# A hybrid layer on one Trainium2 core: queries of the second attention projected with features on partitions

## The chip, the core and the metric

The kernel runs on one core of one Trainium2 chip. The time is that of one execution on the device, in microseconds (us), and the figure compared is the median of several runs. The kernel before has a median of 1133.28 us over 3 runs (1132.96 to 1135.29).

## What is computed

The input x holds 2 batches of 1024 tokens with 512 features, all fp32. Four blocks are added to it in turn, each on a layer-normalised copy:

```python
x = x + attention_a(layernorm(x))
x = x + ffn(layernorm(x))
x = x + attention_b(layernorm(x))
x = x + ffn(layernorm(x))
```

Attention A is a causal differential attention with 16 heads, whose output is filtered along the tokens, scaled per head and projected. The FFN has 8 small experts of 16 inner features, of which each token uses the best 2. Both are left as they are. Attention B is the block in question:

```python
h = _layernorm(X, ln_w, ln_b)
Q, K, V = jnp.split(h @ W_in + b_in, 3, axis=-1)
Q, K = _rope_half(Q), _rope_half(K)        # pairs 2i, 2i+1 of the first 256 features are rotated
A = jnp.sum(_cos_sim(K) * V, axis=-2)      # one row of 512 per batch
Y = (A[:, None, :] * Q) @ W_out + b_out
return Y + X
```

K and V are used only within a token and in a sum over tokens. Q is multiplied by one row A and then by W_out. So the kernel scales the rows of W_out by A once per batch (it calls the result ws) and multiplies q by ws, for which q must have its features on partitions.

## The kernel before

**Tiles.** The 2048 tokens are 16 tiles of 128 (NTILE), 8 for each batch (JT); the 512 features are 4 chunks of 128 (EC). x stays on the chip as x_sb. TensorE takes a stationary operand of 128 x 128 and a moving one; one matmul in fp32 leaves two records in the profile, so a product of 128 x 512 by 512 x 512 (4 matmuls with 512 columns moving) shows as "x8".

**Two stages.** The first stage, up to about 711 us, is attention A without the end of its second half. It isn't touched. The second stage (lines 932 to 1451) is a loop `for t in range(NTILE + 2)` and a tail behind it. In a step t the loop does: the head norm and the output projection of attention A for a later tile (head_norm, mixed, projected; its sums tp_y, yT, z), every few steps products with the filter (common, apart; y), the first FFN of tile t (expert_turn, expert_hidden, expert_gate, expert_back, up; tp_f, xT_f, hr_f, sg_f, atp_f, aT_f, po_f), the layer norm of attention B for tile t-1 (attn_norm, attn_sides, attn_turn; hn_b, tp_b, hT_b) and the projections of attention B for tile t-2 (attn_qk, attn_v, attn_add, accumulate, attn_q). From t=10 it also makes the sums of batch 0 (attn_sum(0)) and one tile of output a step (attn_out; py). From t=13 the second FFN begins, on groups of tiles, and the tail finishes batch 1.

**What sets the order.** The loop stands in `tc.manual_schedule(engines=ordered)`: TensorE, VectorE (DVE) and ScalarE (ACT) execute their instructions in the order in which the Python code writes them. GpSimd (POOL) and SyncE (SP, which issues the loads) may be ordered by the scheduler. Each engine's queue is served in order: an instruction that waits holds up all that stand behind it. Buffers come from pools: six banks of PSUM called "wide" for products, two banks called "tp" for transposes, 8 buffers for QT, 4 for fxT (the turned input of the FFN), 4 for y, one for hT.

**The path of q before.** attn_qk(n, 0) at line 1240 projects q with tokens on partitions (attn_project, line 1236: stationary hT of the tile, moving 512 columns of W_in), adds the bias on VectorE (line 1243) and rotates (rope, lines 1228 to 1231: two products on VectorE, one on POOL, a sum on POOL; pairs lie next to each other, so each product reads every second element). The result qkv_q waits until the end of the step. There attn_q (line 1271) turns it: four transposes on TensorE into a "tp" bank (tp_q, line 970) and one copy on ScalarE into QT (line 975). k takes the same path without the turning. attn_out (line 1296) multiplies QT by ws into py and adds py to x_sb.

**The sums.** attn_sum (line 1279) adds the accumulated row over partitions by TensorE (pc, line 1283), copies it to acol on VectorE (line 1285), and scales W_out by it, two chunks on VectorE (line 1292) and two on ScalarE (line 1294). In step 10 it stands before; that is, behind expert_turn(10), whose last instruction is the copy xT_f on ScalarE (line 1091), and ahead of attn_qk(8, 0). Then follow expert_hidden (hr_f, line 1104), attn_out(0), attn_out(1), attn_v.

Of the kernel before, what the change touches and what calls it, by code (L numbers as in the profile page):

```python
# [11 lines left out]
F32 = mybir.dt.float32  # L12
BF16 = mybir.dt.bfloat16
AF = mybir.ActivationFunctionType
ALU = mybir.AluOpType
# [3 lines left out]
P = 128  # L19
NB, T, E = 2, 1024, 512  # L20
NT = NB * T
JT = T // P
NTILE = NT // P
EC = E // P
# [5 lines left out]
TILE = [b * JT + q + k for b in range(NB) for q in range(2) for k in (0, 4, 2, 6)]  # L30
# [5 lines left out]
def constants():  # L36

    f = np.float32
    t = np.arange(T, dtype=f)

    def tiled(a):
        return np.ascontiguousarray(a.reshape(JT, P, -1).transpose(1, 0, 2).reshape(P, -1))

    inv = (f(1.0) / np.power(f(10000.0), np.arange(0, HD, 2, dtype=f) / f(HD))).astype(f)
    fr = np.outer(t, inv).astype(f)


    r = np.arange(P)
    part = np.where(r // 2 % 2, f(1.0), f(-(HD**-0.5)))[:, None]
    sign = np.where(r % 2, f(1.0), f(-1.0))[:, None]  # L50
    rope_a = np.concatenate([part * np.cos(fr).T[r // 4 % 8], part * sign * np.sin(fr).T[r // 4 % 8]], axis=1).astype(f)

    rot = E // 2
    inv = (f(1.0) / np.power(f(10000.0), np.arange(0, rot, 2, dtype=f) / f(rot))).astype(f)
    fr = (t[:, None] * inv[None, :]).astype(f)
    rope_b = np.concatenate([tiled(np.cos(fr)), tiled(np.sin(fr))], axis=1).astype(f)

    x = np.linspace(0.0, 1.0, T // 2 + 1)  # L60
    taps = np.fft.irfft(np.exp(-0.5 * (x / 0.15) ** 2), n=T)
    lag = (128 * np.arange(JT)[None, :, None] + np.arange(P)[None, None, :] - np.arange(P)[:, None, None]) % T

    block = [taps[lag[:, d]] for d in range(JT)]
    sums = [(block[d] + block[d + 4]) / 2 for d in range(4)]
    parts = [(sums[d] + sums[d + 2]) / 2 for d in range(2)]
    parts += [(sums[d % 4] - sums[(d + 2) % 4]) / 2 for d in range(-1, 2)]
    parts += [(block[d % JT] - block[(d + 4) % JT]) / 2 for d in range(-3, 4)]  # L70
    filt_k = np.concatenate(parts, axis=1).astype(f)


    tri = np.tile(np.tril(np.ones((NE, NE), f), -1).reshape(1, -1), (P, 1))
    return {"c_rope_a": rope_a, "c_rope_b": rope_b, "c_filt": filt_k, "c_tri": tri}


@with_exitstack
def hybrid_layer_kernel(ctx: ExitStack, tc: tile.TileContext, i: dict, out: bass.AP):
    nc = tc.nc  # L80
# [66 lines left out]
    with ExitStack() as sa:  # L147
# [8 lines left out]
        with ExitStack() as sp:  # L156
# [6 lines left out]
            work = sp.enter_context(tc.tile_pool(name="work", bufs=2))  # L163
# [768 lines left out]
        with ExitStack() as sb:  # L932
# [5 lines left out]
            def load_b(name, src, shape):  # L938
                t = wb.tile(shape, F32, tag=name, name=f"{name}_sb")
                nc.sync.dma_start(t, src)  # L940
                return t
# [6 lines left out]
                "rope_b", i["c_rope_b"].rearrange("p (s j f) -> p s j f", s=2, j=JT), [P, 2, JT, E // 4]  # L948
            )
            wob = load_b("wob", i["W_out"].rearrange("(c p) f -> p c f", p=P), [P, EC, E])  # L950
            bias = wb.tile([P, 3 * E], F32, tag="bias", name="bias_sb")
            nc.sync.dma_start(bias, i["b_in"].partition_broadcast(P))
            bout = wb.tile([P, E], F32, tag="bout", name="bout_sb")
            nc.sync.dma_start(bout, i["b_out"].partition_broadcast(P))
            one = wb.tile([P, 1], F32, tag="one", name="one")
# [2 lines left out]
            def wide(name):  # L958
                return ps_w.tile([P, 512], F32, tag="wide", name=name)
# [4 lines left out]
            def w2k(name, tag, bufs=2):  # L964
                return work.tile([P, E], F32, tag=tag, name=name, bufs=bufs)
# [7 lines left out]
            def transposed(dst, src, key):  # L973

                nc.scalar.copy(dst, transposes(src, key))
# [106 lines left out]
            def expert_turn(ns, which):  # L1082
                for n in ns[:2]:
                    expert_scale(n)
                for k, n in enumerate(ns):
                    key = f"f{which}_{n}"
                    xTs[n] = work.tile([P, EC, P], F32, tag="fxT", name=f"xT_{key}", bufs=4)
                    turned = transposes(xns.pop(n), key)
                    if k + 2 < len(ns):
                        expert_scale(ns[k + 2])  # L1090
                    nc.scalar.copy(xTs[n], turned)
# [128 lines left out]

            def rope(t, j, key):

                left = t[:, 0 : E // 2].rearrange("p (f s) -> p f s", s=2)
                cos = rope_b[:, 0, j, :, None].to_broadcast([P, E // 4, 2])
                sin = rope_b[:, 1, j, :]
                ra = work.tile([P, E // 4, 2], F32, tag="ra", name=f"ra_{key}")
                rb = work.tile([P, E // 4, 2], F32, tag="rb", name=f"rb_{key}")
                nc.vector.tensor_mul(ra, left, cos)
                nc.vector.scalar_tensor_tensor(rb[:, :, 0], left[:, :, 1], -1.0, sin, ALU.mult, ALU.mult)
                nc.gpsimd.tensor_mul(rb[:, :, 1], left[:, :, 0], sin)  # L1230
                nc.gpsimd.tensor_add(left, ra, rb)

            def attn_project(n, s):
                pq = wide(f"pq_{'qkv'[s]}{n}")
                for c in range(EC):
                    nc.tensor.matmul(pq, hTs[n][:, c, :], win(c, s), start=(c == 0), stop=(c == EC - 1))  # L1236
                return pq

            def attn_qk(n, s):
                key = f"{'qk'[s]}{n}"  # L1240
                pq = attn_project(n, s)
                t = qkvs[n, s] = w2k(f"qkv_{key}", f"qkv{s}")
                nc.vector.tensor_add(t, pq, bias[:, s * E : (s + 1) * E])
                rope(t, TILE[n] % JT, key)

            def attn_v(n):

# [5 lines left out]
            def attn_add(n):  # L1253

                pq, n2, r0 = qkvs.pop((n, 2))
                rn = rsqrt_step(n2, r0, 1, f"n{n}")
                t = w2k(f"qkv_v{n}", "qkv2", bufs=1)
                nc.vector.tensor_add(t, pq, bias[:, 2 * E : 3 * E])  # L1258
                nc.gpsimd.tensor_mul(t, t, qkvs[n, 1])  # L1259
                qkvs[n, 2] = t, rn  # L1260

            def accumulate(n):
# [4 lines left out]
                    nc.vector.tensor_scalar_mul(acc[b], t, rn)  # L1267
                else:
                    nc.vector.scalar_tensor_tensor(acc[b], t, rn, acc[b], ALU.mult, ALU.add)

            def attn_q(n):
                QTs[n] = work.tile([P, EC, P], F32, tag="QT", name=f"QT_{n}", bufs=8)
                transposed(QTs[n], qkvs[n, 0], f"q{n}")


            group = [0, 1, 2, 3]
            pair = [[n, n + 1] for n in range(4, 16, 2)]
# [1 line left out]
            def attn_sum(b):  # L1279

                pc = wide(f"pc_{b}")
                for c in range(EC):
                    nc.tensor.matmul(pc[:, c : c + 1], acc[b][:, c * P : (c + 1) * P], one, start=True, stop=True)
                col = stat.tile([P, EC], F32, tag="acol", name=f"acol_{b}")
                nc.vector.tensor_copy(col, pc[:, 0:EC])

                if b == 0:
                    wss["both"] = keep.tile([P, JT, E], F32, tag="folded0", name="ws")
                wss[b] = wss["both"][:, EC * b : EC * b + EC, :]
                for c in range(EC):  # L1290
                    if c % 2 == 0:
                        nc.vector.tensor_scalar_mul(wss[b][:, c, :], wob[:, c, :], col[:, c : c + 1])
                    else:
                        nc.scalar.activation(wss[b][:, c, :], wob[:, c, :], AF.Copy, scale=col[:, c : c + 1])

            def attn_out(n):
                py = wide(f"py_{n}")
                for c in range(EC):
                    nc.tensor.matmul(py, QTs[n][:, c, :], wss[n // JT][:, c, :], start=(c == 0), stop=(c == EC - 1))  # L1299
                nc.vector.tensor_add(x_sb[:, n, :], x_sb[:, n, :], py)  # L1300
                ns = group if n < 4 else pair[n // 2 - 2]
                group_moments(ns, ns.index(n))

            with tc.manual_schedule(engines=ordered):
                for t in range(NTILE + 2):

                    def due(what, n, *args, listed=False):
                        if 0 <= n < NTILE:
                            what([n] if listed else n, *args)
# [41 lines left out]
                    if mixing and t > 2:  # L1351
                        due(up, t - 1, 0, listed=True)
                        due(attn_norm, t - 1)
                    due(attn_qk, t - 2, 1)
                    if not mixing:
                        due(expert_back, t - 1, 0, listed=True)
                    if t == 0:
                        expert_turn([2], 0)
                    if t > 2:
                        due(expert_turn, t, 0, listed=True)  # L1360
                    if t == 10:
                        attn_sum(0)
                    if t == 14:
                        expert_turn(group, 1)
                    if t == 17:
                        expert_turn(pair[0], 1)
                        group_norm(pair[1])
                    due(attn_qk, t - 2, 0)
                    if not mixing:
                        due(up, t - 1, 0, listed=True)  # L1370
                        if t != 15:
# [7 lines left out]
                        attn_norm(t - 1)  # L1379
                    if t == 10:  # L1380
                        attn_out(0)
                    if 10 <= t < 17:
                        attn_out(t - 9)
                    due(attn_sides, t - 1)
# [15 lines left out]
                    due(attn_add, t - 2)  # L1400
                    if turned is not None:
                        projected(turned)
                    due(attn_q, t - 2)
                    if t == 14:
                        expert_gate(group, 1)
                    if t == 13:
# [79 lines left out]
```

## Time and profile before

| | us |
|---|---|
| median of 3 runs | 1133.28 |
| the profiled execution | 1133.31 |
| its span, from first to last instruction | 1131.2 |
| second stage, from 711 to the end of the span | 420 |

| group of the second stage (from 741 us on) | records | busy us |
|---|---|---|
| pq_q, line 1236 | 128 | 57.7 |
| tp_q, line 970 | 64 | 9.6 |
| tp_y, line 970 | 44 | 6.8, with 1.7 idle ahead, released by ACT QT |
| py, line 1299 | 128 | 57.0 |

How to read it. The mean granted clock of TensorE is 0.992 of full. "Busy" of TensorE adds up records of which the ends are modelled; consecutive matmuls overlap, so what one costs is read from the distance between starts. A line of the timeline has the start in us, the busy time, the engine, the line of the kernel, the operation, output and inputs with their shapes, a count, and in brackets the idle time ahead of it with what ended it. A line of the windows has the window, its length, the busy time of TensorE, its weight loads (PEld), VectorE, ScalarE and POOL with counts, the granted clock, the share of the DMA engines and GB/s.

### The profile page before, as it was taken

The page shows a single profiled execution, that of the slowest core. Times are in us where ns is not written, and L with a number is a line of the kernel's source. Part 1 is how long each engine was busy: PE and PEld are TensorE (multiplying, and loading weights), DVE is VectorE, ACT ScalarE, POOL GpSimd, SP SyncE. Part 2 cuts the span into 40 slices and gives each one's busy share as a digit, 9 for nine tenths or more (in the row PEclk, how much of TensorE's full clock was granted, in tenths as well). Part 3 has the DMA queues.
Part 4 walks back from the last instruction along what each step waited for, and adds up shares of the span by engine and source line. Part 5 has one row for each costly group of instructions (what it writes and reads, how often), then busy time and mean ns, then how long its engine had stood idle before and what let it go on. Part 6 is the DMA issues. An engine that isn't in the chain of part 4 may idle for free.

```text
span 1131.2 us, 23505 instructions
## 1 busy us (share of the span) xinstructions
PE 1072.7 (95%) x8680; PEld 732.0 (65%) x8680; DVE 930.8 (82%) x2046; ACT 763.7 (68%) x2010; POOL 436.6 (39%) x689
## 2 busy tenths in 40 slices
PE   6999999999999999999999989799999999999997
PEld 5777777777767787777777655445545455554554
DVE  5799999999889889989999987577787777758576
ACT  3698988989989889999999866243434333443533
POOL 1346446455354544634544662123223223223200
PEclk9999999999999999999999999989999999999999
DMA  5212222211301101110110611200000000001002
GB/s 178 80 43 68 81 85 63 76 34 53 118 16 39 46 17 35 48 44 15 40 43 18 226 72 39 113 0 1 1 0 1 1 1 1 1 1 38 1 19 93
DMA packets 33345, 52.19 MB, mean 46 GB/s; under 512 B 6480, under 2 KB 11088, under 8 KB 33104
## 3 DMA queue, kind: packets, MB, share of 16 engines
q1 hardware_dynamic: 33072, 50.44, 14.0%
q8 instruction: 69, 1.13, 0.4%
q14 instruction: 44, 0.36, 0.1%
q10 hardware_dynamic: 160, 0.26, 0.1%
HBM read 23.42 MB, written 6.29 MB: 26 GB/s over the span
## 4 chain that ended last, share of the span: by engine, by line
PE 62%; DVE 20%; ACT 12%; issue 4%; POOL 1%; DMA 1%; SPq 0%; DVEq 0%; POOLq 0%; ACTq 0%
PE s L499 8%; ACT p L531 7%; PE bank L355 7%; DVE least L522 6%; PE dtp L590 5%; PE bank L617 5%; PE py L1299 5%; PE pq_q L1236 5%; DVE p L566 4%; PE pq_v L1236 4%; PE pq_k L1236 4%; PE z L1040 3%; PE y L990 2%; PE hr_f L1104 2%; DVE least L514 2%
## 5 line engine op out<-in xcount | busy, mean ns | idle before, releaser
L531 ACT ACTIVATE p<-s,least 128x640 f32<-128x640 f32 (+7 forms) x512 | 378.1, 745 | 37.7 <-DVE least L522 23.2
L522 DVE TENSOR_REDUCE least<-s 128x1 f32<-128x896 f32 (+5 forms) x384 | 244.1, 678 | 27.1 <-PE s L499 26.4
L566 DVE SCALAR_TENSOR_TENSOR p<-p,ratio,p 128x1024 f32<-128x1024 f32 (+7 forms) x256 | 226.9, 921 | 3.8 <-POOL ratio L559 3.8
L592 ACT COPY dt<-dtp 128x512 f32<-128x512 f32 x288 | 169.0, 587 | 38.4 <-PE dtp L590 35.2
L590 PE MATMUL dtp<-ident,p 128*128 128x128 f32 x1152 | 180.2, 279 | 10.9 <-ACT dt L592 5.1
L499 PE MATMUL s<-keys,qk 32*128 32x128 f32 (+3 forms) x1408 | 184.1, 438 | 0.7 <-ACT p L531 0.7
L590 PEld LDWEIGHTS dtp<-ident,p 128*128 128x128 f32 x1152 | 129.5, 141 | 36.1 <-ACT dt L592 16.1
L514 DVE TENSOR_REDUCE least<-s 128x1 f32<-128x1024 f32 (+1 forms) x96 | 115.8, 1213 | 23.3 <-PE s L499 23.3
L499 PEld LDWEIGHTS s<-keys,qk 32*128 32x128 f32 x1408 | 101.7, 185 | 39.4 <-issue 26.2
L559 POOL TENSOR_TENSOR ratio<-ratio,inverse 128x2 f32<-128x2 f32 (+1 forms) x144 | 27.9, 194 | 236.0 <-DVE inverse L557 211.2
L355 PE MATMUL bank<-xnT,wqk 128*128 128x256 f32 x472 | 114.5, 385 | 3.1 <-ACT raw L366 2.4
L551 POOL TENSOR_TENSOR ratio<-sums,neg_lam 128x2 f32<-128x2 f32 (+1 forms) x144 | 72.5, 503 | 115.2 <-ACT p L531 114.8
L531 ACT ACTIVATION_READ_ACCUMULATOR p<-s,least 128x1 f32 x512 | 104.9, 205 | 0.0
L499 PE MATMUL s<-swapped 32*128 32x128 f32 (+2 forms) x896 | 104.3, 344 | 0.0
L355 PEld LDWEIGHTS bank<-xnT,wqk 128*128 128x128 f32 x472 | 85.0, 190 | 18.0 <-ACT raw L366 5.7
L499 PEld LDWEIGHTS s<-swapped 32*128 32x128 f32 x896 | 70.4, 184 | 9.6
L476 PE MATMUL s<-eye 128*128 128x256 bf16 (+1 forms) x320 | 76.6, 256 | 0.0
L617 PE MATMUL bank<-dt,v 128*32 128x128 f32 x2304 | 69.5, 274 | 1.9 <-ACT v L387 1.1
L617 PEld LDWEIGHTS bank<-dt,v 128*32 128x32 f32 x2304 | 60.9, 110 | 8.2 <-ACT v L387 4.6
L400 POOL TENSOR_TENSOR other<-other,rope_a_sb 128x512 f32<-128x512 f32 x30 | 62.9, 2095 | 0.0
L1259 POOL TENSOR_TENSOR qkv_v<-qkv_v,qkv_k 128x512 f32<-128x512 f32 x16 | 20.3, 1269 | 108.4 <-DVE qkv_v L1258 107.3
L379 PE MATMUL bank<-wval,xnT 128*128 128x128 f32 x448 | 60.5, 283 | 0.5
(222 smaller groups left out, 1785.5 us busy)
## 6 DMA issues: line engine op xcount, KB each, us to landing
other<-raw SPq DMA_DIRECT2D x64, 128.0 KB, 2.1
xin<-in_query SPq DMA_DIRECT2D x16, 256.0 KB, 2.9
keys<-qk SPq DMA_DIRECT2D x64, 64.0 KB, 1.9
swapped<-keys SPq DMA_DIRECT2D x32, 128.0 KB, 2.3
x_sb<-in_query SPq DMA_DIRECT2D x16, 256.0 KB, 6.4
out_dram<-x_sb SPq DMA_DIRECT2D x16, 256.0 KB, 2.1
swapped<-qk SPq DMA_DIRECT2D x30, 128.0 KB, 2.3
wqk<-in_w_qk SPq DMA_DIRECT2D x8, 256.0 KB, 2.7
```

The costliest lines, as they stand in the source:

```text
L355: nc.tensor.matmul(pp, wqk[:, part, c, :], xnT[b, half][:, c, t0 : t0 + 256], start=(c == 0), stop=(c == EC - 1),)
L476: nc.tensor.matmul(s[mm][:, d0 : d0 + width], eye[:, 0, :], eye[:, 1 : 1 + width // P, :].rearrange("p k q -> p (k q)"), start=first, stop ...
L499: nc.tensor.matmul(s[mm][:, c0 : c0 + w], q[r0 : r0 + 32, j * P - back : (j + 1) * P - back], k[r0 : r0 + 32, s0 - back : s0 - back + w], ...
L514: nc.vector.tensor_reduce(least[n][:, e[0] : e[-1] + 1 : e[-1] - e[0] or 1, mm], s[mm].rearrange("p (g k) -> p g k", g=g), AX.X, ALU.min,)
L522: nc.vector.tensor_reduce(least[n][:, e, mm : mm + 1], s[mm][:, c0 : c0 + w], AX.X, ALU.min)
L531: nc.scalar.activation(ps[mm][:, c0 : c0 + w], sv, AF.Exp, bias=low, scale=-1.0, accum_out=sums[n][mm][:, e : e + 1],)
L551: nc.gpsimd.tensor_mul(ratio[:, w], first, neg_lam.to_broadcast([P, w.stop]))
L566: nc.vector.scalar_tensor_tensor(ps[0][:, c0 : c0 + w], ps[1][:, c0 : c0 + w], ratio[:, k : k + 1], ps[0][:, c0 : c0 + w], ALU.mult, ALU.add,)
L590: nc.tensor.transpose(tp[:, k * P : (k + 1) * P], d[:, c0 : c0 + P], ident)
L592: nc.scalar.copy(dt[:, 4 * half : 4 * half + 4, :], tp.rearrange("p (k q) -> p k q", k=4))
L617: nc.tensor.matmul(po[32 * g : 32 * g + 32, c0 : c0 + P], vals[n // 2 % 2][:, k, 64 * (n % 2) + 32 * h : 64 * (n % 2) + 32 * h + 32], dt[: ...
L1236: nc.tensor.matmul(pq, hTs[n][:, c, :], win(c, s), start=(c == 0), stop=(c == EC - 1))
```

## The change

On the host, the columns of each third of W_in, the entries of b_in and the rows of W_out are permuted: of the first 256 features those with even numbers come first, then those with odd numbers. The sums over features are the same in any order, and the pairs of the rotation now are two contiguous halves.

q is projected turned: for each of 4 chunks of output features 4 matmuls have a 128 x 128 piece of W_in stationary and hT moving with 128 columns. The result has features on partitions. VectorE adds the bias, now one value for each partition (bias_q), straight into QT, and the rotation (a new function turn, which rope also calls) works there on two whole chunks, with a new constant rope_q of cosines and sines with features on partitions (1 MB). The transposes tp_q, the copy into QT and the buffers of qkv_q are gone.

The calls are moved with it: attn_q(t-2) stands where attn_qk(t-2, 0) stood, except in step 10, where it stands behind attn_out(0), which frees the QT buffer of tile 0. In that step attn_sum(0) moves up to the place directly behind k, ahead of expert_back and expert_turn. The first FFN has 2 buffers of fxT in place of 4, and the second FFN uses the 4 buffers of y for the same thing.

```diff
-            bias = wb.tile([P, 3 * E], F32, tag="bias", name="bias_sb")
-            nc.sync.dma_start(bias, i["b_in"].partition_broadcast(P))
+            rope_q = load_b("rope_q", i["c_rope_q"].rearrange("p (s t) -> p s t", s=2), [P, 2, T])
+            bias_q = load_b("bias_q", i["b_in"][0:E].rearrange("(c p) -> p c", p=P), [P, EC])
+            bias = wb.tile([P, 2 * E], F32, tag="bias", name="bias_sb")
+            nc.sync.dma_start(bias, i["b_in"][E : 3 * E].partition_broadcast(P))
...
-                    xTs[n] = work.tile([P, EC, P], F32, tag="fxT", name=f"xT_{key}", bufs=4)
+                    tag, bufs = (("fxT", 2), ("y", 4))[which]
+                    xTs[n] = work.tile([P, EC, P], F32, tag=tag, name=f"xT_{key}", bufs=bufs)
...
-                left = t[:, 0 : E // 2].rearrange("p (f s) -> p f s", s=2)
-                cos = rope_b[:, 0, j, :, None].to_broadcast([P, E // 4, 2])
+                left = t[:, 0 : E // 2].rearrange("p (s f) -> p s f", s=2)
+                cos = rope_b[:, 0, j, None, :].to_broadcast([P, 2, E // 4])
+                turn(left, cos, rope_b[:, 1, j, :], key)
+
+            def turn(left, cos, sin, key):
+                ra = work.tile([P, 2, E // 4], F32, tag="ra", name=f"ra_{key}")
+                rb = work.tile([P, 2, E // 4], F32, tag="rb", name=f"rb_{key}")
                 nc.vector.tensor_mul(ra, left, cos)
-                nc.vector.scalar_tensor_tensor(rb[:, :, 0], left[:, :, 1], -1.0, sin, ALU.mult, ALU.mult)
-                nc.gpsimd.tensor_mul(rb[:, :, 1], left[:, :, 0], sin)
+                nc.vector.scalar_tensor_tensor(rb[:, 0, :], left[:, 1, :], -1.0, sin, ALU.mult, ALU.mult)
+                nc.gpsimd.tensor_mul(rb[:, 1, :], left[:, 0, :], sin)
                 nc.gpsimd.tensor_add(left, ra, rb)
...
+            def attn_q(n):
+                pq = wide(f"pq_q{n}").rearrange("p (c q) -> p c q", c=EC)
+                for f in range(EC):
+                    for c in range(EC):
+                        nc.tensor.matmul(
+                            pq[:, f, :],
+                            win_qk[:, c, f * P : (f + 1) * P],
+                            hTs[n][:, c, :],
+                            start=(c == 0),
+                            stop=(c == EC - 1),
+                        )
+                QT = QTs[n] = work.tile([P, EC, P], F32, tag="QT", name=f"QT_{n}", bufs=8)
+                nc.vector.tensor_add(QT, pq, bias_q[:, :, None].to_broadcast([P, EC, P]))
+                j = TILE[n] % JT
+                cos, sin = (rope_q[:, k, j * P : (j + 1) * P] for k in range(2))
+                turn(QT[:, 0:2, :], cos[:, None, :].to_broadcast([P, 2, P]), sin, f"q{n}")
...
-            def attn_q(n):
-                QTs[n] = work.tile([P, EC, P], F32, tag="QT", name=f"QT_{n}", bufs=8)
-                transposed(QTs[n], qkvs[n, 0], f"q{n}")
...
-                    due(attn_qk, t - 2, 1)
+                    due(attn_k, t - 2)
+                    if t == 10:
+                        attn_sum(0)
                     if not mixing:
                         due(expert_back, t - 1, 0, listed=True)
...
                     if t > 2:
                         due(expert_turn, t, 0, listed=True)
-                    if t == 10:
-                        attn_sum(0)
...
-                    due(attn_qk, t - 2, 0)
+                    if t != 10:
+                        due(attn_q, t - 2)
...
                     if t == 10:
                         attn_out(0)
+                        attn_q(t - 2)
                     if 10 <= t < 17:
                         attn_out(t - 9)
...
-                    due(attn_q, t - 2)
...
+    perm = np.r_[0 : E // 2 : 2, 1 : E // 2 : 2, E // 2 : E]
+    for name, axis, parts in (("W_in", 1, 3), ("b_in", 0, 3), ("W_out", 0, 1)):
+        arrays[name] = np.take(arrays[name], np.concatenate([E * k + perm for k in range(parts)]), axis=axis)
```

## The prediction, made before the changed kernel was run

> **What bounds the kernel now.** I read the share of each engine first, then the chain that ended last, then the busy time in windows, then single stretches of the timeline.
>
> ```profile
> PE 1072.7 (95%) x8680; PEld 732.0 (65%) x8680; DVE 930.8 (82%) x2046; ACT 763.7 (68%) x2010; POOL 436.6 (39%) x689
> ...
> PE 62%; DVE 20%; ACT 12%; issue 4%; POOL 1%; DMA 1%; SPq 0%; DVEq 0%; POOLq 0%; ACTq 0%
> ```
>
> These are averages over the span. The change touches only what runs after 711 us, so that part needs its own windows (window, length, then PE, PEld, DVE, ACT, POOL busy, granted clock):
>
> ```profile
> 740.50:987.80 247.30, 245.60 (x782) 124.24 (x782) 186.91 (x589) 94.65 (x283) 71.28 (x107) 1.00 0.00 1
> 987.80:1073.80 86.00, 81.01 (x308) 44.67 (x306) 56.77 (x176) 35.02 (x90) 23.74 (x33) 1.00 0.04 13
> 1073.80:1131.20 57.40, 50.92 (x190) 27.89 (x190) 40.51 (x128) 21.65 (x51) 0.00 (x0) 0.97 0.15 55
> ```
>
> From 740.5 to 987.8 (steps t=2 to t=13) TensorE is busy for 99% of the time: what TensorE issues there is the time, and work taken off ScalarE or VectorE is worth nothing by itself. After 987.8 about 5 of 86 us are idle, so chains through VectorE and ScalarE decide at some places; the tail follows whatever happens earlier.
>
> **Part 1: the projection turned, against transposing q.** Before, pq_q is 8 records of 128x512, 429 ns from one to the next in this stretch (3.43 us), and tp_q is 4 records of 128x128 at 109 ns (0.435 us). After, pq_q is 32 records of 128 columns. The first stage has the same form (fp32, 128x128 weights, 128 columns moving), in the timeline (start, busy, ...):
>
> ```profile
> 25.76 7.31 PE L379 MATMUL values<-wval,xnT 128*128 128x128 f32 x64
> 32.90 1.89 PE L355 MATMUL qk<-xnT,wqk 128*128 128x256 f32 x8
> ```
>
> The group of 64 starts at 25.76 and the next at 32.90: 7.14 / 64 = 111.6 ns each, so 32 take 3.57 us. Per tile: +0.14 for pq_q, -0.435 for tp_q, net -0.295 us where both lie on the path. Bounds of the record: 109 ns (the transposes) to 116 ns (the 136-column hr_f), 3.49 to 3.71 us; I take the row of the same form. [...]
>
> **Part 2: the wait on the QT copy at some step ends.** Where the next step begins without products for y, the end of a step looks so (here step 9):
>
> ```profile
> 898.68 0.60 PE L970 MATMUL tp_q<-ident,qkv_q 128*128 128x128 f32 x4
> 899.12 0.27 PE L1161 MATMUL atp_f<-ident,sg_f 128*128 128x128 f32 x1
> 899.96 0.66 PE L970 MATMUL tp_y<-ident,yn 128*128 128x128 f32 x4 [0.57 <-ACT QT L975]
> 900.45 1.02 PE L1174 MATMUL po_f<-wup_sb,aT_f 128*128 128x512 f32 x2
> 901.31 3.60 PE L1236 MATMUL pq_k<-win_qk,hT_b 128*128 128x512 f32 x8
> ```
>
> tp_y needs one of two transpose banks and waits 0.57 us for ScalarE's copy out of tp_q. From 898.68 to pq_k are 2.63 us; without tp_q and its copy atp_f, aT copy, po_f remain, about 1.48 us: -1.15. This occurs three times (5 to 6, 9 to 10, 10 to 11; "tp_y <- ACT QT" holds 1.7 us in all). The other ends save only tp_q.
>
> **Part 3: what is moved at t=10.** The column sums of batch 0 (attn_sum(0): pc, acol, ws) now stand before expert_turn, so ScalarE's queue has its two ws ahead of the xT_f copy. That adds a wait: behind ws stand xT_f, xb_b and the gate's exponentials, and TensorE's hr_f waits for xT_f, with py, pq_q, pq_v queued behind hr_f. Before:
>
> ```profile
> 905.66 0.57 ACT L1091 COPY xT_f<-tp_f 128x512 f32<-128x512 f32 x1
> 908.37 0.15 DVE L1285 COPY acol<-pc 128x4 f32<-128x4 f32 x1
> 908.55 1.33 ACT L1294 ACTIVATE ws<-wob_sb,acol 128x512 f32<-128x512 f32 x2 [2.33 <-DVE acol L1285]
> 909.51 1.09 PE L1104 MATMUL hr_f<-wdr_sb,xT_f 128*128 128x136 f32 x8
> ```
>
> xT_f was done 3.3 us before hr_f, and pq_q (3.43 us, also moved, now behind py of tile 0) covered the wait for acol, which is last in VectorE's chain of yn, x+po, moments, hn, k's bias and rope. Let T = 898.68, the end of step 9. After, that chain starts 0.5 us sooner (no tp_q, no QT copy): acol T+9.19, ws T+9.37 to T+10.6, xT_f to T+11.2, hr_f T+11.24. TensorE has po_f, pq_k, pc and tp_f, all done at T+6.15: idle for 5.1 us. From there 0.93 (hr_f), 3.43 (py 0), 3.57 (pq_q), 3.43 (py 1) put pq_v at T+22.60, against 917.30 = T+18.62: **+3.98 us**, the gains of that step's beginning already in it. The gate's chain on VectorE, 4 us later too, ends about T+27.6, before z ends at T+29.9, so nothing more is late.
>
> **Part 4: the clock after that idle time.** The only comparable gap of this stage is just before 737.74:
>
> ```profile
> 737.74 2.07 PE L1174 MATMUL po_f<-wup_sb,aT_f 128*128 128x512 f32 x2 [2.83 <-ACT aT_f L1164]
> ...
> 740.47 4.57 PE L1236 MATMUL pq_k<-win_qk,hT_b 128*128 128x512 f32 x8
> ```
> ```profile
> 736.00:737.00 1.00, 0.00 (x0) 0.00 (x0) 1.00 (x2) 1.00 (x4) 0.77 (x1) 0.50 0.00 0
> 741.00:742.00 1.00, 1.00 (x2) 0.33 (x1) 1.00 (x2) 0.00 (x0) 0.00 (x0) 0.50 0.00 0
> 743.00:744.00 1.00, 1.00 (x3) 0.38 (x2) 0.46 (x4) 0.74 (x3) 0.00 (x0) 1.00 0.00 0
> ```
>
> The granted clock (the column 0.50 and 1.00) falls to one half after idle times of 1.16 and 2.83 us and is back at 742.4, two stretches of 3.41 us later; po_f took 2.07 us, pq_k 4.57 against 3.6 elsewhere. The changes of clock in this trace lie on one grid of 3.41 us; it fell after stretches busy for 44 and 47%, and held at 67%. Laid on that grid at every phase, a gap of 5.1 us leaves the half rate on for 1.8 to 5.2 us of the work behind it (until a busy stretch has ended), and half of that is lost: 0.9 to 2.6 us, an estimate; I take the middle, **+1.7**. [...]
>
> **Part 5: contiguous halves and the rest.** The strided pairs become halves. VectorE's second product does not end before POOL's:
>
> ```profile
> 1025.47 0.70 POOL L1230 TENSOR_TENSOR rb_k<-qkv_k,rope_b_sb 128x128 f32<-128x128 f32 x1 [5.93 <-DVE qkv_k L1243]
> 1025.77 0.55 DVE L1229 SCALAR_TENSOR_TENSOR rb_k<-qkv_k,rope_b_sb 128x128 f32<-128x128 f32 x1
> ```
>
> It ends 0.15 us behind POOL's, here as at 746.14 (1.39 us long, beside a POOL addition). Gain per rope between 0 and 0.25 us (POOL's 0.70 falling to about VectorE's 0.42 for twice the elements); a loss has no row for it, as the element count stays. I take 0, since TensorE hides VectorE in these steps; only t=10 and two later chains would pass it on: -0.85 in all at 0.25. The QT addition has the size and PSUM source of L1243 (0.68 us), and takes its place one for one; between 0.42 and 0.69. Sixteen ScalarE copies of 0.58 go: off the path except as counted. Loads: SP's queue gets rope_q (1 MB) and bias_q ahead of bias and bout, bias is 0.25 MB less: +0.75 MB, 2 us at the 400 GB/s of that stretch. rope_b is issued at 710.03 and bout lands near 720; bout is first needed at 736, bias at 745, rope_q at 749. Cost 0, up to 16 us of cover; without it, 2 us. POOL's memset of the ones now stands behind the last folds (715.3) and is needed at 719.7: 0.
>
> **Sum against the profiled execution.** Steps to 9: 7 x -0.435, -0.72 (end of 5), 8 x +0.14: -2.64. t=10: +3.98, clock +1.7. End of 10: -1.15. t=11, 12: 2 x -0.295. t=13, 14, 16: +0.14 each (tp_q at 987.84 lies beside a VectorE chain to 991.94, and at 15 and 16 beside the wait for hT_b, so nothing is won there). t=15: 0, VectorE's chain to 1031.97 decides. t=17: -0.14. Last step: tp_q and its copy stand before aT (1068.81 to 1070.36): -0.68. Total **+0.9 us**. The profiled execution took 1133.31 us (span 1131.2 and 2.1 around it), 0.03 above the median 1133.28: forecast **1134.2 us**. All else saves 4.8 us; t=10 takes 5.7 back.
>
> **Rivals.** A difference of 0.2% is 2.27 us, about what a measurement of this kernel can tell from none: under 1131.0 or over 1135.55.
> *Slower:* the stall at t=10 is longer and colder. If VectorE's chain doesn't start sooner the stall is 4.48, and if two grid stretches run cold, as at 735.6 to 742.4, hr_f and py lose 2.6 to 3.4: -4.78 + 4.48 + 2.6 to 3.4 = +2.3 to +3.1, about 1136.0. It decides once stall and clock together take more than 7.05 us. For it: that cold stretch. Against: a 5 us gap with full work behind it leaves at most one and a half stretches cold in most phases.
> *Doesn't do what it says:* narrow records cost more beside the wider weights traffic. At 116 ns: +0.14 on some 14 tiles, +2.0, so 1136.2; at 120.9 tp_q's saving is eaten: +4.1, 1138.3. Against: the 64 records at 111.6.
> *Faster:* the stall is mostly missing, because acol comes sooner (rope without its lock, ropes 0.25 shorter) and the grid phase costs nothing. No stall: 1128.5; a stall of 2 us, warm: about 1130.5. For it: two free parameters at their ends. Against: xT_f stands behind ws in the queue, so it can't be earlier than acol.
>
> **Chances.** Forecast 0.50 (own range 1132.0 to 1135.5), slower rival 0.20, narrow records 0.10, faster rival 0.20. So faster 0.20, same 0.50, slower 0.30. Range 1129.8 to 1137.0: it leaves out a missing stall (some 0.07) and the dear end of the narrow records with the coldest stall (some 0.08).
>
> **What would show it.** In the profile after: 512 records of pq_q with 111.6 ns between starts, no tp_q and no QT copy; a step of 20.5 us where 20.82 stood; no wait of tp_y on QT; before the hr_f of t=10 an idle of 5 us released by ACT xT_f, itself waiting for acol; a clock of 0.50 in the stretch behind it. No such idle, or starts of 116 ns and more, would make the prediction wrong.

## The result and the profile after

The changed kernel has a median of 1136.41 us (22 runs, 1134.10 to 1138.66), the kernel before, measured beside it, 1134.55 us (22 runs, 1132.46 to 1135.53). The ratio is 1.0021 with a 95% interval of 1.0015 to 1.0027: slower by 2.4 us, between 1.7 and 3.1. The forecast of 0.9 us has the sign right and is too small, and the time lies inside the range. By the prediction's own border for telling a change from none, 2.27 us, the result lies just on the slower side, to which it gave 0.30, and the interval reaches across that border. The profiled execution took 1134.10 us, the shortest of the 22, with a span of 1132.0.

From the page of the changed kernel, the busy time of each engine:

```profile
PE 1071.0 (95%) x9000; PEld 760.8 (67%) x9000; DVE 929.5 (82%) x2046; ACT 755.8 (67%) x1994; POOL 436.5 (39%) x689
```

TensorE is busy for 1.7 us less than before, ScalarE for 8 us less, and the run is longer: there must be new idle time. The waits of TensorE from 741 us on (engine, instruction, what it waited for; us in total, times, longest) name the first, here two lines of before and then two of the changed kernel:

```profile
PE tp_y L970 <- ACT QT L975: 1.7, 3, 0.6
...
PE tp_f L970 <- ACT aT_f L1164: 0.6, 1, 0.6
```

```profile
PE hr_f L1109 <- ACT xT_f L1096: 4.8, 1, 4.8
...
PE tp_f L974 <- ACT aT_f L1169: 1.0, 1, 1.0
```

The line of before, "tp_y <- ACT QT" with 1.7 us, is gone, as forecast. In its place stand one wait of 4.8 us, and one of 1.0 where 0.6 stood (tp_f behind aT_f). The waits of pq_k for hT_b have grown too, from 0.5 to 2.0 us in all: the transposes of q used to stand in them, and the prediction counted on no gain there. Step 10 in the timeline of TensorE (start, busy, instruction, idle time ahead of it):

```profile
893.88 0.27 PE L1166 MATMUL atp_f<-ident,sg_f 128*128 128x128 f32 x1
...
899.72 0.64 PE L974 MATMUL tp_f<-ident,xn_f 128*128 128x128 f32 x4
905.12 2.18 PE L1109 MATMUL hr_f<-wdr_sb,xT_f 128*128 128x136 f32 x8 [4.77 <-ACT xT_f L1096]
907.09 5.10 PE L1318 MATMUL py<-ws,QT 128*128 128x512 f32 x8
912.02 3.73 PE L1257 MATMUL pq_q<-hT_b,win_qk 128*128 128x128 f32 x32
```

Step 9 ends at 893.88, and hr_f starts 11.24 us later, where the prediction put it. But then 8 records of hr_f take 1.97 us from start to start in place of 0.93, and py 4.93 in place of 3.43: that is the clock. In windows of 1 us of the same kernel (window, length, PE, PEld, DVE, ACT, POOL busy, granted clock):

```profile
902.00:903.00 1.00, 0.00 (x0) 0.00 (x0) 0.96 (x3) 0.00 (x0) 0.68 (x1) 1.00 0.00 0
...
904.00:905.00 1.00, 0.00 (x0) 0.00 (x0) 0.70 (x2) 1.00 (x3) 0.03 (x1) 0.50 0.00 0
...
909.00:910.00 1.00, 1.00 (x3) 0.47 (x2) 0.00 (x0) 0.00 (x0) 0.00 (x0) 0.50 0.00 0
```

In windows of 0.25 us the half clock begins at 903.3, 1.8 us before hr_f, and ends at 910.1: two stretches of 3.4 us. Why xT_f is late stands in the same timeline on the other engines:

```profile
903.07 0.15 DVE L1304 COPY acol<-pc 128x4 f32<-128x4 f32 x1
903.26 1.34 ACT L1313 ACTIVATE ws<-wob_sb,acol 128x512 f32<-128x512 f32 x2 [2.79 <-DVE acol L1304]
904.50 0.56 ACT L1096 COPY xT_f<-tp_f 128x512 f32<-128x512 f32 x1
```

TensorE had issued pc by 899.72. acol waits in VectorE's queue behind the bias and rotation of k until 903.07, ws behind acol, xT_f behind ws, hr_f behind xT_f. ScalarE was idle for 2.79 us ahead of ws, and the copy xT_f, whose input tp_f was there by about 900.4, ran only behind ws, at 904.50.

The second place is step 14, in the same timeline:

```profile
993.23 0.66 PE L974 MATMUL tp_f<-ident,xn_g 128*128 128x128 f32 x4 [1.02 <-ACT aT_f L1169]
...
997.70 4.29 PE L1257 MATMUL pq_q<-hT_b,win_qk 128*128 128x128 f32 x32
```

pq_q takes 4.13 us from start to start here, against 3.57 in other steps: a stretch at half clock from 995.4 to 998.8, which the kernel before doesn't have.

### The profile page after: what moved, and what is told of

Same layout as the page of the kernel before. It is cut to its first block, busy times and chain, and to the rows that moved or that the text cites. A ratio compares the mean times of both kernels' runs of the same rounds, so it can differ in the third digit from the quotient of the medians.

```text
span 1132.0 us, 24133 instructions
## 1 busy us (share of the span) xinstructions
PE 1071.0 (95%) x9000; PEld 760.8 (67%) x9000; DVE 929.5 (82%) x2046; ACT 755.8 (67%) x1994; POOL 436.5 (39%) x689
## 4 chain that ended last, share of the span: by engine, by line
PE 61%; DVE 21%; ACT 12%; issue 4%; POOL 1%; DMA 1%; DVEq 0%; SPq 0%; POOLq 0%
PE s L501 8%; ACT p L533 7%; PE bank L357 7%; DVE least L524 6%; PE dtp L592 6%; PE bank L619 5%; PE pq_q L1257 5%; PE py L1318 5%; DVE p L568 4%; PE pq_v L1244 4%; PE pq_k L1244 4%; PE z L1044 3%; PE hr_f L1109 2%; DVE least L516 2%; PE y L994 2%
```

## The experiments

**e1: a ninth buffer for QT**, and with it the old order of step 10.

```diff
-                QT = QTs[n] = work.tile([P, EC, P], F32, tag="QT", name=f"QT_{n}", bufs=8)
+                QT = QTs[n] = work.tile([P, EC, P], F32, tag="QT", name=f"QT_{n}", bufs=9)
...
                     due(attn_k, t - 2)
-                    if t == 10:
-                        attn_sum(0)
...
                         due(expert_turn, t, 0, listed=True)
+                    if t == 10:
+                        attn_sum(0)
...
-                    if t != 10:
-                        due(attn_q, t - 2)
+                    due(attn_q, t - 2)
...
                         attn_out(0)
-                        attn_q(t - 2)
```

> The changed kernel with 9 QT buffers in place of 8, so that q of tile 8 keeps its place in step 10 and attn_sum(0) goes back behind expert_turn: the turned projection stays, the order of step 10 is that of before. My theory (the turned projection saves 0.295 us a tile and some waits, 4.8 us in all, and the order of step 10 takes back 4.0 us of idle time and about 1.7 to 2.5 us of half clock): 4.5 to 5.7 us faster than before, ratio about 0.9955; in the trace hr_f of step 10 does not wait for xT_f and the granted clock stays full around it. Rival 1 (the narrow records cost what the transposes saved, the order of step 10 is harmless): within 1 us of the changed kernel, some 2 us slower than before.

Measured: ratio 0.9941 (0.9928 to 0.9954), 6.7 us faster than before, with an interval of 5.2 to 8.2; that is above the 4.5 to 5.7 expected, and from step 3 on its trace is 4.3 us shorter than that of before. Its step 10:

```profile
907.95 1.09 PE L1109 MATMUL hr_f<-wdr_sb,xT_f 128*128 128x136 f32 x8
908.88 7.03 PE L1318 MATMUL py<-ws,QT 128*128 128x512 f32 x16
```

pq_q, issued at 904.29, covers the time until xT_f and ws are there; nothing waits, and hr_f and py run at full clock. Rival 1 falls: the turned projection gains at least what it should, and the order of step 10 gave it back.

**e2: only the order of step 10**, in the kernel before.

```diff
                     due(attn_qk, t - 2, 1)
+                    if t == 10:
+                        attn_sum(0)
...
-                    if t == 10:
-                        attn_sum(0)
...
-                    due(attn_qk, t - 2, 0)
+                    if t != 10:
+                        due(attn_qk, t - 2, 0)
...
                         attn_out(0)
+                        attn_qk(t - 2, 0)
```

> The kernel before with nothing but the order of step 10 changed: attn_sum(0) directly behind k, q of tile 8 behind attn_out(0). q is still projected with tokens on partitions and transposed. My theory: about 4.4 us of idle time ahead of hr_f plus 1.7 to 2.5 us at half clock, so 5.2 to 7 us slower than before, ratio about 1.0053. Rival 1 (order harmless): within 0.5 us of before.

Measured: ratio 1.0049 (1.0037 to 1.0061), 5.6 us slower.

```profile
911.80 2.18 PE L1104 MATMUL hr_f<-wdr_sb,xT_f 128*128 128x136 f32 x8 [4.21 <-ACT xT_f L1091]
913.77 5.44 PE L1299 MATMUL py<-ws,QT 128*128 128x512 f32 x8
```

The same wait and the same slow records, without any turned q. From pq_k of step 10 to that of step 11 it takes 7.21 us longer than before; the other steps stay within 0.01 us, except the first two (0.4 us up, 0.4 down) and the tail (1.0 us less; the clock is full there in e2, and at one half for 3.4 us in the kernel before), which also vary between profiles of one kernel.

**e3: the wait filled with work nobody reads.**

```diff
                         due(expert_turn, t, 0, listed=True)
+                    if t == 10:
+                        fill = wide("fill")
+                        for c in (0, 1, 2, 3, 0):
+                            nc.tensor.matmul(fill, hTs[8][:, c, :], win(c, 1), start=True, stop=True)
```

> The changed kernel with 5 matmuls of 128x512 that nobody reads (10 records, 4.3 us) between tp_f and hr_f of step 10: TensorE waits as long for xT_f, but is busy. My theory (two separate costs, idle time and half clock): hr_f starts when it did, 11.2 us behind the end of step 9, but its 8 records take 0.93 us and py 0 3.43 us from start to start; 1.7 to 2.5 us faster than the changed kernel, so about 0 to 0.5 us slower than before. Rival 2 (the half clock there is not caused by the idle time, or costs nothing on the path): like the changed kernel, about 2.2 us slower than before.

Measured: ratio 0.9991 (0.9982 to 1.0000), 1.0 us faster than before, so about 3.4 us faster than the changed kernel: the sign and the mechanism as expected, the size above it.

```profile
902.43 4.46 PE L1385 MATMUL fill<-win_qk,hT_b 128*128 128x512 f32 x10
907.36 1.19 PE L1109 MATMUL hr_f<-wdr_sb,xT_f 128*128 128x136 f32 x8 [0.47 <-ACT xT_f L1096]
908.39 3.60 PE L1318 MATMUL py<-ws,QT 128*128 128x512 f32 x8
```

hr_f starts 11.24 us behind the end of step 9 (896.12), to the hundredth as in the changed kernel, but py now takes 3.43 us (pq_q follows at 911.82). From pq_k of step 10 to that of step 11 it is 4.08 us more than before: that is the idle time alone. The changed kernel has 6.52 there; the difference, 2.44 us, is the clock alone (2.88 and 2.93 with e6 and e7, below). So the traces account for 2.4 to 2.9 of the 3.4 us. Rival 2 falls.

**e4: only the sums back**, q of tile 8 still behind attn_out(0), 8 buffers.

```diff
                     due(attn_k, t - 2)
-                    if t == 10:
-                        attn_sum(0)
...
                         due(expert_turn, t, 0, listed=True)
+                    if t == 10:
+                        attn_sum(0)
```

> The changed kernel with attn_sum(0) back behind expert_turn, q of tile 8 still behind attn_out(0). My theory (both moves cost: without pq_q as a cover TensorE waits for ws itself): xT_f is early, hr_f runs at once, and py of tile 0 waits about 3.7 us for ws; pq_v 21.2 us behind the end of step 9 instead of 22.6 warm, the clock as cold as before: 1.4 us faster than the changed kernel, about 0.8 us slower than the kernel before. Rival 3 (only ScalarE's queue, xT_f behind ws, is to blame): no stall at all, 4 us or more faster than before.

Measured: ratio 0.9999 (0.9991 to 1.0008), within 1 us of before on either side.

```profile
903.76 1.19 PE L1109 MATMUL hr_f<-wdr_sb,xT_f 128*128 128x136 f32 x8 [0.70 <-ACT xT_f L1096]
907.23 6.72 PE L1318 MATMUL py<-ws,QT 128*128 128x512 f32 x8 [2.27 <-DVE ws L1311]
```

The wait has moved from hr_f to py and is in two pieces, 0.70 and 2.27 us, yet the clock fell to one half as well (py 6.55 us, pq_q follows at 913.78). The wait is shorter than the 3.7 us expected, 2.97 in all. With the sums back, ScalarE copies xT_f at 903.14, ahead of ws at 906.03, so its queue was what held hr_f; but it isn't only that queue (rival 3): without pq_q as a cover TensorE waits for ws in this order too.

**e5: only the layout in halves**, in the kernel before: the permutation of W_in, b_in and W_out, and in rope

```diff
-                left = t[:, 0 : E // 2].rearrange("p (f s) -> p f s", s=2)
+                left = t[:, 0 : E // 2].rearrange("p (s f) -> p s f", s=2)
```

with cos, ra and rb in the same order.

> The kernel before with only the layout changed: columns of W_in, b_in and rows of W_out evens first, the rotation on contiguous halves; q still with tokens on partitions and transposed. My theory (the products are as long, and TensorE hides them in most steps): the rotation's second product on POOL stays at 0.69 to 0.70 us, within 0.3 us of before. Rival 4 (strided operands were the cost): POOL's product falls towards 0.42 us and the kernel gains 0.5 to 0.85 us.

Measured: ratio 0.9997 (0.9985 to 1.0008). The product on POOL, from the view of the tile rb_k of this kernel (duration in ns: least, median, longest):

```profile
L1230 POOL TENSOR_TENSOR rb_k<-qkv_k,rope_b_sb x16: 459/689/695, 747.3 to 1057.2; 128x128 f32<-128x128 f32 x16
```

In the kernel before the median is 694 ns; VectorE's product beside it has 544 ns, 551 before. Contiguous halves gain 5 to 7 ns an operation, and no difference in the time is seen. Rival 4 falls.

**e6, e7 and e8: other profiles of the same kernels**, the changed one twice and the one before once, without an edit.

> The changed kernel once more, for a second profile. Its runs lie between 1134.1 and 1138.7 us and the profiled one was the shortest. My theory: in a longer run the same instructions wait for the same things, step by step with the same lengths, and the difference lies in stretches of 3.41 us at half clock (begin of the second stage, step 10, the turning of four tiles in step 14, the tail). Rival 5: some wait on a load or on another engine is longer.

> The changed kernel a third time, for another phase of the clock's grid. My theory: idle ahead of hr_f in step 10 again 4.8 us within 0.2 us, the half clock behind it 1.8 to 5.2 us long. Rival 5: the idle time itself varies by more than 0.5 us.

> The kernel before once more, for a second profile: its runs fall into two groups, near 1132.8 and near 1135.2 us. My theory: the groups differ in stretches at half clock around the begin of the second stage and in step 14, not in waits; step 10 stays at full clock. Rival 5: a wait differs.

Measured: 1136.48, 1136.75 and 1134.58 us. The idle time ahead of hr_f is 4.77, 4.78 and 4.78 us in the three profiles of the changed kernel. From hr_f to pq_q of step 10 it takes 6.90, 7.33 and 7.39 us in place of 4.36 at full clock: 2.5, 3.0 and 3.0 us lost. Of the work from hr_f on, 4.98, 5.84 and 5.95 us ran at half clock; in e7 that is beyond the 5.2 expected.

Step 14 has its stretch at half clock in all three, and in e1, e3 and e4 as well; in none of the four profiles with q transposed (before, e2, e5, e8). Rival 5 falls for the steps. Where e6 and e8 differ from the first profile of their kernel was expected only in part: 1.9 of e6's 2.4 us lie ahead of step 3. There the untouched first stage ends 1.1 us later; it has 3.4 us at half clock near 671 us, which the first profile of the changed kernel has not. e8 starts its second stage 0.9 us later; its first stage has 6.8 us at half clock from 316 us, which the first profile of before has not. It is then 0.4 us slower at the beginning, faster by as much in the step behind, and 0.4 us slower in the tail. Step 14 is the same in both profiles of before, not a difference as expected. Which stretches the other runs had was not recorded, so their spread from 1132.5 to 1135.5 is not fully explained.

**e9: the waits of step 14 filled with work nobody reads**, on top of e1.

```diff
+                    if which and ns is group:
+                        if k == 0:
+                            junk = wide("junk")
+                        cols = 512 if k == 0 else 256
+                        nc.tensor.matmul(
+                            junk[:, 0:cols], hTs[12][:, k, :], win_qk[:, k, E : E + cols], start=True, stop=True
+                        )
                     turned = transposes(xns.pop(n), key)
```

> The kernel with 9 QT buffers, with four matmuls that nobody reads (one of 512 columns, three of 256) ahead of the four turnings of the group in step 14, where TensorE waits 0.5 to 1.0 us each time. My theory (with the transposes of q gone, the first of these waits grew from 0.6 to 1.0 us, a stretch of 3.41 us falls below about half busy and the clock goes to one half for the next): full clock from 980 to 1020 us, the distance from pq_k of step 14 to that of step 15 shrinks from 28.3 to about 26.6 us, 1.6 us faster than with 9 buffers alone, ratio to before about 0.993. Rival 6 (something else makes step 14 longer, such as VectorE's chain): the distance stays at 28.3 us, ratio 0.994 to 0.995.

Measured: ratio 0.9934 (0.9920 to 0.9948); the intervals of e1 and e9 overlap, so the runs alone do not separate them. The traces do: from pq_k of step 14 to that of step 15 it takes 26.71 us against 28.33 in e1, and the clock is full throughout.

```profile
987.89 0.66 PE L974 MATMUL tp_f<-ident,xn_g 128*128 128x128 f32 x4 [0.17 <-ACT aT_f L1176]
...
991.95 3.74 PE L1264 MATMUL pq_q<-hT_b,win_qk 128*128 128x128 f32 x32
```

The last turning starts 8.73 us behind pq_k, as in e1 (8.72): the junk delays nothing, and pq_q is back at 3.57 us. Rival 6 falls.

**e10: the waits of step 14 filled with q itself**, also on top of e1.

```diff
                     turned = transposes(xns.pop(n), key)
+                    between(k)
...
-                        expert_turn(group, 1)
+                        expert_turn(group, 1, lambda k: attn_q_part(t - 2, k))
```

(attn_q_part makes the 4 matmuls of one chunk; attn_q then only adds the bias and rotates.)

> The kernel with 9 QT buffers, and in step 14 the 16 matmuls of q of tile 12 stand in four parts between the four turnings of the group, in TensorE's waits. My theory: the 2.6 us of waiting and the 1.6 us of half clock of step 14 are both filled with work that has to be done anyway; if nothing else is late, 4 us faster than with 9 buffers alone, ratio to before about 0.990. Rival 6 (VectorE's chain of steps 14 and 15 decides): 1 us or less gained, ratio 0.993 to 0.994.

Measured: ratio 0.9914 (0.9902 to 0.9927), median 1125.39 us, 9.8 us faster than before: the best version here, ahead of both kernels. From pq_k of step 14 to that of step 15 are 24.46 us, 3.87 less than in e1, as expected; nothing else is late. The clock is full there. The first wait of the step, 1.03 us ahead of the first turning, is still there, as q stands only behind it.

```profile
988.17 1.06 PE L1260 MATMUL pq_q<-hT_b,win_qk 128*128 128x128 f32 x8
989.06 0.60 PE L974 MATMUL tp_f<-ident,xn_g 128*128 128x128 f32 x4
```

## Why the prediction was right in kind and short in size

The starts of pq_k cut the second stage into steps. The table has the time between them, as a difference to the first profile of the kernel before; "forecast" are the terms of the sum:

| from pq_k of step | forecast | changed | e6 | e7 | what it shows |
|---|---|---|---|---|---|
| 3 to 10 | -3.50 | -3.28 | -3.28 | -3.28 | narrow records, tp_q and the QT wait |
| 10 to 11 | +3.98 and +1.7 | +6.52 | +6.96 | +7.01 | idle time and clock |
| 11 to 15 | -0.31 | +0.66 | +0.88 | +0.90 | step 14 |
| 15 to 17 | +0.14 | +0.13 | +0.14 | +0.14 | pq_q alone |
| 17 to the end | -0.82 | -0.67 | -0.87 | -0.97 | last transposes |

**Part 1 holds.** pq_q takes 3.58 us (882.07 to 885.65), 32 records of 111.8 ns; a step lost 0.30 us, forecast 0.295. Four narrow records take 447 ns here and a wide one 429, as the row of the first stage said.

**Part 2 holds** to 0.1 us: 0.89 and 0.90 where 1.01 was forecast (pq_q's 0.14 taken off 1.15), because from atp_f to pq_k it took 1.59 us and not 1.48.

**Part 3 holds**: 4.08 us (e3, without the clock) against 3.98, and hr_f to the hundredth. That the two moves of step 10 are the cause is shown by e1 and e2, and e3 parts the loss into wait and clock. That xT_f waits behind ws in ScalarE's queue is read in the trace and borne out by e4, where xT_f is ahead of ws and hr_f waits 0.70 us; e4 adds that moving q alone would have cost much of it too.

**Part 4 was mis-sized.** The forecast took 1.7 us, the middle of 0.9 to 2.6; 2.5 to 3.0 were lost. The failed step is "until a busy stretch has ended". In e7 the half clock began at 906.4 and hr_f at 907.28, so TensorE was busy for 74% of that first cold stretch, and still a second one passed before the clock came back, at 913.2; in the first profile and e6 also two, and in e4 two although the first was busy for 80%. The first cold stretches of e7 and e4:

```profile
906.41:909.82 3.41, 2.54 (x9) 2.31 (x10) 0.45 (x2) 1.54 (x3) 1.27 (x1) 0.50 0.00 0
```
```profile
906.54:909.95 3.41, 2.72 (x4) 1.20 (x5) 0.94 (x2) 1.53 (x3) 1.52 (x2) 0.50 0.00 0
```

So the loss is half of 6.8 us less the time from the fall of the clock to hr_f. This is the size that the slower rival gave (2.6 to 3.4), without its other half: VectorE's chain did start sooner. The prediction's shares were a partial reading as well: its 44% is 46% up to the fall at 735.59 (1.57 of 3.41 us), and where it has "held at 67%", in the same trace, in the first stage, the clock fell at 670.7 after a stretch that was 67% busy:

```profile
667.33:670.74 3.41, 2.29 (x24) 1.49 (x23) 3.31 (x6) 2.76 (x11) 2.71 (x3) 1.00 0.00 0
```

**A term was missing.** Step 14 was put at +0.14, with tp_q's share not won since VectorE's and ScalarE's chain hides it. With the clock full that is right for the sum: e9 has -0.29 from step 11 to 15, forecast -0.31 (step 13 gains 0.30 and step 14 loses 0.60 there, where +0.14 stood for each). But the time that TensorE no longer spends on tp_q comes back as a longer wait there, 1.0 us in place of 0.6, and in all six profiles with this step (the changed kernel three times, e1, e3, e4) the clock falls in it. The stretch before the fall, with the boundaries of each profile, is busy for 44 to 53%; here those of e6 and e1:

```profile
994.81:998.22 3.41, 1.54 (x10) 1.07 (x11) 1.90 (x4) 3.41 (x7) 1.42 (x2) 1.00 0.00 0
```
```profile
990.31:993.72 3.41, 1.81 (x13) 1.10 (x12) 0.77 (x2) 3.41 (x7) 1.35 (x2) 1.00 0.00 0
```

Before, with the boundaries counted on from 742.42 in steps of 3.413 us (the changes of its clock at 670.74, 735.59, 742.42 and 1124.71 lie 19, 2 and 112 such steps apart), the emptiest stretch of this place holds 63% (58% in e5), and the clock stays:

```profile
991.59:995.00 3.41, 2.14 (x14) 1.30 (x12) 2.48 (x6) 3.02 (x6) 1.42 (x2) 1.00 0.00 0
```

With boundaries 0.4 to 0.8 us later it would hold only 1.76 us, so a phase in which the kernel before falls too is possible; none of its profiles shows one. The price, against e9's 0.60 from pq_k of step 14 to 15, is 0.95, 1.17 and 1.19 us in the three profiles and 1.6 in e1.

**The sum.** 0.9, plus 1.15 (2.85 in place of 1.7), plus 1.1 for step 14, is 3.15 us, just above the measured 1.7 to 3.1. From step 3 on the profiles bear this out: the table's columns add up to 3.4 to 3.8 us, against 1.2 forecast there, and 0.4 less against e8. Ahead of step 3 the three profiles of the changed kernel are on average 1.6 us sooner than the two of before, of which 0.3 were forecast. 0.9 of it lies in the untouched first stage, whose last transposes start anywhere from 709.5 to 712.7 us in the twelve traces of this study. Its stretches at half clock go with that: with none the transposes start at 709.48 (the first profile of the changed kernel), with 3.4 us near 671 at 710.55 to 710.74 (before, e5, e6, e7), with 6.8 us near 316 at 710.61 and 710.85 (e10, e9), with both at 711.55 to 712.72 (e1 to e4, e8). Compared among equals in this, e6 and e7 are 0.6 and 0.4 us ahead of before at step 3, and 3.2 and 3.5 us behind it at the end. Why the clock falls in the first stage of some executions and not of others stays open, and so does which of them the 22 runs had.

**Part 5 holds**: halves gain nothing that these runs show (e5), and no wait on a load stands in the waits of the changed kernel. The "lock" of the faster rival is a word for this in the trace of before: 30 of VectorE's 32 second products end 0.14 to 0.16 us behind an operation of POOL that runs beside them, 27 of them after 0.54 or 0.55 us; the two that started with POOL idle (827.26 and 933.81) took 0.28.

## What to carry to other kernels

When work is taken from the engine that bounds, look at the places where it also served as a cover: here q's projection hid the way from pc over acol to ws (without it hr_f waited 4.77 us, in e1 not at all), and the transposes of q hid part of a chain in step 14 (a wait of 1.02 us in place of 0.6). A wait of TensorE can cost its length and then the clock, here 4.1 and 2.4 us in step 10; work that has to be done anyway, put into the wait, won 3.87 us of both in step 14 (e10), and a single buffer (the ninth QT) can be what allows it. A move that a buffer count forces is priced as a change of its own.

## What the hardware showed that I had not expected

In the second stage the half clock had two different edges. In step 14 stretches of 3.4 us that were 44 to 53% busy were followed by the fall, those of 58 and 63% were not; but once the clock had fallen, in step 10, a stretch of 74 or 80% didn't bring it back, so that an idle time of 4.8 us went with 6.8 us at half clock in each of three profiles. In step 14, where the cold stretch itself was over 90% busy, it lasted 3.4 us; in the tail of the kernel before a cold stretch of 78% was enough, so the edge upwards is not sharp by this measure. In the first stage the busy share didn't decide: the clock fell near 671 us after stretches of 59 to 79% (67% before), and stayed at one half near 316 us behind cold stretches of 90 to 96% (95% in e8). Those of the tail (before) and near 316 us (e8):

```profile
1124.71:1128.12 3.41, 2.67 (x4) 0.57 (x2) 2.17 (x4) 0.00 (x0) 0.00 (x0) 0.50 1.00 371
```
```profile
316.11:319.52 3.41, 3.24 (x18) 2.47 (x20) 3.22 (x7) 2.67 (x7) 2.96 (x9) 0.50 0.00 0
```

What else the clock goes by was not found. In step 14 it fell although no wait there is longer than 1.02 us in the first profile of the changed kernel and in e1, and 1.04 us in e6.
